# Layer 1's experts in two halves of the node tiles, with routing and last stage set between them

## The chip, the cores and the metric

The kernel runs on one core of a Trainium2 chip. The metric is the device time of one execution in microseconds. A kernel of this size has one instruction stream for each engine (TensorE, called PE; VectorE, DVE; ScalarE, ACT; GpSimd, POOL; and SyncE, SP, which issues most DMAs). Each engine works through its own stream in order and waits on semaphores for the others.

## The reference

A two-layer graph network over 6250 nodes of 256 features and 100,000 edges. Each layer adds a graph convolution and a linear attention, and then a mixture of experts. Only the last of these, layer 1's experts, has changed much:

```python
# x: (6250, 256) after layer 1's graph attention and mixer
xn = _layernorm(x)
gate_logits = xn @ gate_w + gate_b                 # 16 experts
topk_vals, topk_idx = lax.top_k(gate_logits, 2)
topk_w = softmax(topk_vals)
h = relu(einsum('bsh,ehf->bsef', xn, w1) + b1)     # 256 -> 512
expert_out = einsum('bsef,efh->bseh', h, w2) + b2  # 512 -> 256
moe = sum(topk_w * expert_out[chosen two])
y = xn + moe
x = x + (y - mean(y)) / sqrt(var(y) + EPS) * gamma + beta
```

The kernel computes only the two chosen experts of each node, in float32.

## The kernel before

Nodes lie in 49 tiles of 128 (the last has 106). Layer 1's experts are the function `expert_pairs`, in three stages one after the other.

*Routing* (`dispatch`, with `finals`, `logits` and `put`) goes over 13 groups of 2, 3 and then 4 node tiles. `finals` loads the running sum `xl` and the transposed rows `xm`, multiplies `xm` by the mixer's `kvm` (tile `mix`, L1908), divides the attention sums `acc` by their denominators (L1914), adds everything and stores the new x to `xs2_d` in DRAM. `logits` normalizes it into `xn` (one copy for each of the two choices), transposes it on PE (L131, evicted by ACT at L133) and multiplies by the router (tile `lp`, L387). `put` searches the two largest logits (`top`, `ti`, L400 and L401), counts with a scan and two products (tile `pp`, L436 and L437) which row of its expert's area each node gets (`d_pi`, L443), and scatters the rows with POOL's indirect DMA into `xs_d` (`f_xs` in the profile, L448): two scatters for each node tile. `logits` of one group is written down ahead of `put` of the group before it; the order of the engines' instructions in this stage is a scheduler's. `xn` has three buffers. During the stage SP also loads the second weights `w2` of all 16 experts (8.4 MB). At its end `dispatch` makes a table: for every expert tile of 128 rows its expert and its first row. It then writes 128 zero rows behind each expert's rows (L498): eight addresses are read into registers at once on SP, eight on ACT.

*Experts* (`stages`, `some`) go over these tiles, in an order written out by hand (`tc.manual_schedule()`). For tile i, `load` fetches the expert's first weights `w1` (512 KB, five buffers) and the rows `xt` five tiles ahead; `turn` transposes the rows two tiles ahead; `first_product` makes the 512 hidden values `hT` (16 matmul records at L1983, evicted half by ACT, L1988, half by DVE, L1991) one tile ahead; `second_product` makes `y` (8 records, L1999), DVE adds b2 and the input (L2002, L2004), and POOL scatters the result into `ys_d` (`f_ys`, L332), to the row of its node and choice. `b2` lies in `acc`, over the columns of the first 16 node tiles. Between the tiles a small generator reads `xs2_d`, adds beta and writes it back. The first 104 tiles always run; three conditional blocks of 3 follow, each run only if there are so many tiles.

*Last stage* (L2030 to L2043): in seven groups of 7 node tiles, both results and x + beta are loaded, added, normalized on DVE, scaled by gamma and written out.

Layer 0's experts use the same `dispatch` with one choice and groups of 2, 5 and 7 tiles.

Of the kernel before, what the change touches and what calls it, by code (L numbers as in the profile page):

```python
# [52 lines left out]
def gps_kernel(ctx, tc, x, src, dst, edge_weight, g0_W, g0_b, m0_WqT, m0_WkvT, m0_WpT, m0_bp,  # L53
# [276 lines left out]
    def give_back(name, ys_d, xt, y):  # L330

        st = nc.gpsimd.indirect_dma_start(  # L332
            out=ys_d, in_=y, in_offset=None,
            out_offset=bass.IndirectOffsetOnAxis(ap=xt.bitcast(I32)[:, C:C + 1], axis=0),
            bounds_check=ys_d.shape[0] - 1, oob_is_err=False)
        tc.declare_no_dep(st.ins, group=name + "y", reason="every result has a row of its own")
        tc.add_to_no_dep_group(name + "y", st.ins)

    def results(t, ys_d, k, t0, n):

        whole = n if t0 + n < NT else n - 1
        if whole < n:
            nc.vector.memset(t[:, whole, :], 0.0)
        r0 = (k * NT + t0) * P
        if whole:
            nc.sync.dma_start(t[:, :whole, :], ys_d[r0:r0 + whole * P, :].rearrange(
                "(t p) c -> p t c", p=P))
        if whole < n:
            nc.sync.dma_start(t[:LAST, whole, :], ys_d[r0 + whole * P:r0 + whole * P + LAST, :])

    def dispatch(name, fb, fw, pps, ne, nk, sizes, rw, rb, ns, xs_d, finals):
# [21 lines left out]
        def logits(t0, n):  # L373
            x_ = finals(t0, n)
            xn = [fw.tile([P, bt, rw_], F32, name=f"xn{k}", bufs=3) for k in range(nk)]
            layernorm(fw, x_, xn[0][:, :, :C], n)
            for k in range(nk):
                if k:
                    nc.scalar.copy(xn[k][:, :n, :C], xn[0][:, :n, :C])
                nc.vector.tensor_copy(xn[k].bitcast(I32)[:, :n, C], ids[:, k, t0:t0 + n])  # L380
                if nk == 2:
                    nc.vector.memset(xn[k][:, :, C + 2], 1.0 - k)
# [5 lines left out]
            lg = fw.tile([P, bt, ne], F32, name="lg")  # L388
# [4 lines left out]
        def put(t0, n, xn, lg, turn):  # L393
            ti = fw.tile([P, bt, 8], U32, name="ti")
# [59 lines left out]
        held = logits(*groups[0])  # L454
        for j, g in enumerate(groups):
            ahead = logits(*groups[j + 1]) if j + 1 < len(groups) else None
            put(*g, *held, j % 2)
            held = ahead
# [598 lines left out]
    xs2_d = tc.dram_tile([P, NT, C], F32, name="xs2_d")  # L1057
# [797 lines left out]
    def expert_pairs(ne, nk, hid, w1_d, b1_d, w2_d, b2_d, rw_d, rb_d, ns, xs_d, ys_d):  # L1855
        lead, step = 104, 3
        nf = hid // P
        wn = 2 * hid
        with ExitStack() as ctx1:
            fp = ctx1.enter_context(tc.tile_pool(name="f1", bufs=1))  # L1860
            oi = [fp.tile([1, ns], I32, name=f"own{n}") for n in (1, wn, nf, C)]
            adr = fp.tile([1, ns], I32, name="adr")
# [4 lines left out]
                                             ap=[[0, P], [1, C]]))  # L1867
            with tc.tile_pool(name="f1w", bufs=1) as wp_:
# [10 lines left out]
                with tc.tile_pool(name="f1a", bufs=2) as fw, tc.tile_pool(name="f1b", bufs=1) as fb, \  # L1879
                        tc.tile_pool(name="f1p", bufs=2, space=PSUM) as pps:  # L1880
                    rw = fb.tile([P, 2, ne], F32, name="rw")
                    nc.scalar.dma_start(rw, rw_d.rearrange("(c p) o -> p c o", p=P))
                    rb = fb.tile([P, ne], F32, name="rb")
                    nc.scalar.dma_start(rb, bass.AP(tensor=rb_d.tensor, offset=rb_d.offset,
                                                    ap=[[0, P], [1, ne]]))
                    b1 = fb.tile([ne, hid], F32, name="b1")
# [5 lines left out]
                    accv = acc.rearrange("p (t c) -> p t c", c=CR)  # L1892
                    rd = fb.tile([P, NT, 4], F32, name="rd")
                    nc.vector.tensor_scalar(rd, accv[:, :NT, C:], 1e-16, None, op0=OP.add)
                    nc.vector.reciprocal(rd, rd)

                    def finals(t0, n):
                        xl = fw.tile([P, 4, C], F32, name="xl", bufs=3)
                        nc.sync.dma_start(xl[:, :n, :], xs1_d[:, t0:t0 + n, :])
                        for t in range(t0, t0 + n, 2):  # L1900
                            m = min(2, t0 + n - t)
                            xm = fw.tile([P, 2, 2, P], F32, name="xm", bufs=4)
                            for i in range(m):
                                nc.sync.dma_start(xm[:, i], xnT_d[t + i])
                            mix = pps.tile([P, 2, C], F32, name="mix")
                            for i in range(m):
                                for h in range(2):
                                    nc.tensor.matmul(mix[:, i, h * P:(h + 1) * P], xm[:, i, h, :],  # L1908
                                                     kvm[:, h, :], start=True, stop=True)
                            i = t - t0  # L1910
                            nc.vector.tensor_add(xl[:, i:i + m, :], xl[:, i:i + m, :], mix[:, :m, :])
                        for t in range(t0, t0 + n):
                            av = accv[:, t, :C].rearrange("p (k d) -> p k d", k=4)
                            nc.vector.tensor_tensor(  # L1914
                                av, av, rd[:, t, :, None].to_broadcast([P, 4, 64]), op=OP.mult)
                        nc.vector.tensor_add(xl[:, :n, :], xl[:, :n, :], accv[:, t0:t0 + n, :C])
                        nc.sync.dma_start(xs2_d[:, t0:t0 + n, :], xl[:, :n, :])
                        if t0 >= 8:
                            for _ in range(2):
                                next(w2s, None)  # L1920
                        return xl[:, :n, :]

                    own, first, nt = dispatch("f1", fb, fw, pps, ne, nk, (2, 3) + (4,) * 11, rw, rb, ns, xs_d,
                                              finals)
                    for _ in w2s:
                        pass
                    for o, n in zip(oi, (1, wn, nf, C)):
                        nc.vector.tensor_scalar(o, own, float(n), None, op0=OP.mult)
                    nc.vector.tensor_copy(adr, first)
                    nc.vector.tensor_copy(used, nt)  # L1930
                with tc.tile_pool(name="f1x", bufs=1) as fb, tc.tile_pool(name="f1v", bufs=2) as fv, \
                        tc.tile_pool(name="f1q", bufs=2, space=PSUM) as pps:
                    b2 = acc[:, :ne * C]
                    nc.scalar.dma_start(b2, bass.AP(tensor=b2_d.tensor, offset=b2_d.offset,
                                                    ap=[[0, P], [1, ne * C]]))
                    bet = spread(fb, f1_beta, "bet")

                    def with_beta(t0):
                        xb = fb.tile([P, CH, C], F32, name="xb")
                        nc.sync.dma_start(xb, xs2_d[:, t0:t0 + CH, :])  # L1940
                        yield
                        nc.vector.tensor_tensor(xb, xb, bet[:, None, :].to_broadcast([P, CH, C]),
                                                op=OP.add)
                        yield
                        nc.sync.dma_start(xs2_d[:, t0:t0 + CH, :], xb)
                        yield

                    betas = (None for t0 in range(0, NT, CH) for _ in with_beta(t0))
# [140 lines left out]
```

## Time and profile before

| | |
|---|---|
| median of 7 runs | 3434.54 us (3425.16 to 3440.21) |
| the profiled execution | 3435.69 us, of it the span 3433.8 us |
| PE busy in the span | 2235.0 us (65%), 10357 instructions |
| DVE busy | 2217.7 us (65%), 6283 |
| POOL busy | 1938.0 us (56%), 1895 |
| ACT busy | 658.6 us (19%), 1775 |
| mean granted PE clock | 0.811 |
| HBM | 431.21 MB read, 116.99 MB written |

Times in the profile are counted from the first instruction. A line such as "L448 POOL" is line 448 of the kernel before. The profile gives, for groups of instructions, their busy time, the mean of one, and the idle time of their engine just before them with the instruction that ended it; in such rows "out<-in" names the tiles written and read. The "chain" is followed back from the last instruction through whatever released each step. PE's clock is granted by the chip between 0.50 and 1.00 of full speed and is given as a mean over a stretch. A float32 matmul shows as two records, a transpose as one. The DMA share is the mean busy share of the core's 16 DMA engines.

### The profile page before, as it was taken

The page shows a single profiled execution, that of the slowest core. Times are in us where ns is not written, and L with a number is a line of the kernel's source. Part 1 is how long each engine was busy: PE and PEld are TensorE (multiplying, and loading weights), DVE is VectorE, ACT ScalarE, POOL GpSimd, SP SyncE. Part 2 cuts the span into 40 slices and gives each one's busy share as a digit, 9 for nine tenths or more (in the row PEclk, how much of TensorE's full clock was granted, in tenths as well). Part 3 has the DMA queues.
Part 4 walks back from the last instruction along what each step waited for, and adds up shares of the span by engine and source line. Part 5 has one row for each costly group of instructions (what it writes and reads, how often), then busy time and mean ns, then how long its engine had stood idle before and what let it go on. Part 6 is the DMA issues. An engine that isn't in the chain of part 4 may idle for free. (4 is left out here: it accounts for less than half of the span.)

```text
span 3433.8 us, 40629 instructions
## 1 busy us (share of the span) xinstructions
PE 2235.0 (65%) x10357; PEld 1708.9 (50%) x10357; DVE 2217.7 (65%) x6283; ACT 658.6 (19%) x1775; POOL 1938.0 (56%) x1895
## 2 busy tenths in 40 slices
PE   4677789985555364767455556555555564999970
PEld 3444567764434253656233334333333453899970
DVE  6365666666666673665478888788888764344448
ACT  2212112210000011422011111111111132344420
POOL 0477777777777433710677777777777055222220
PEclk9989999997677655988788888888877665999995
DMA  6734434433333325466655555555554384777757
GB/s 199 210 115 122 117 117 126 128 114 99 95 96 95 99 60 134 153 212 181 189 165 160 161 160 167 165 167 159 169 164 122 103 285 144 241 254 251 249 183 246
DMA packets 323374, 547.51 MB, mean 159 GB/s; under 512 B 83881, under 2 KB 208274, under 8 KB 322995
## 3 DMA queue, kind: packets, MB, share of 16 engines
q1 hardware_dynamic: 224556, 285.05, 26.1%
q0 software_dynamic: 91104, 245.32, 24.7%
q10 hardware_dynamic: 7464, 14.32, 1.4%
q8 instruction: 94, 1.54, 0.2%
q14 instruction: 156, 1.28, 0.1%
HBM read 431.21 MB, written 116.99 MB: 160 GB/s over the span
## 5 line engine op out<-in xcount | busy, mean ns | idle before, releaser
L300 POOL DMA_INDIRECT h<-h_d,idx x782 | 785.7, 1005 | 404.7 <-issue 229.8
L300 POOL DMA_INDIRECT xg<-xw_d,idx x782 | 803.4, 1027 | 364.5 <-issue 222.7
L1547 PE MATMUL ps<-h,S 128*128 128x260 f32 x1564 | 416.4, 429 | 426.6 <-DVE S L1541 426.6
L852 PE MATMUL ps<-xg,S 128*128 128x256 f32 x1564 | 489.6, 458 | 268.5 <-DMA xg<-xw_d,idx 197.5
L1547 PEld LDWEIGHTS ps<-h,S 128*128 128x128 f32 x1564 | 329.7, 215 | 520.8 <-DVE S L1541 463.4
L852 PEld LDWEIGHTS ps<-xg,S 128*128 128x128 f32 x1564 | 334.0, 228 | 393.0 <-issue 184.2
L332 POOL DMA_INDIRECT f_ys<-y,xt x175 | 184.8, 1056 | 361.6 <-DVE y L2004 273.4
L860 DVE SCALAR_TENSOR_TENSOR acc<-ps,in,acc 128x256 f32 x392 | 188.3, 480 | 281.8 <-PE ps L852 280.6
L448 POOL DMA_INDIRECT f_xs<-xn,d_pi x147 | 152.4, 1037 | 194.0 <-DVE d_pi L443 80.5
L1536 DVE TENSOR_TENSOR h<-h,exi 128x2048 f32<-128x2048 f32 x98 | 223.0, 2276 | 57.1 <-ACT exi L1495 57.1
L850 DVE TENSOR_SCALAR S<-iota,lo,wt 128x128 f32<-128x128 f32 x782 | 240.4, 356 | 0.1
L1991 DVE TENSOR_SCALAR h<-hT,b1T 128x128 f32<-128x128 f32 x214 | 75.1, 351 | 218.1 <-ACT h L1988 217.7
L1983 PE MATMUL hT<-xTt,w 128*128 128x128 f32 x1712 | 209.9, 276 | 0.3 <-ACT xTt L133 0.3
L1999 PE MATMUL y<-w,h 128*128 x856 | 202.1, 379 | 0.0
L1983 PEld LDWEIGHTS hT<-xTt,w 128*128 128x128 f32 x1712 | 201.0, 193 | 0.6 <-ACT xTt L133 0.5
L1404 PE MATMUL p<-ST,hw 128*32 128x512 f32 x392 | 177.4, 606 | 34.7 <-DVE ST L1399 16.9
L1999 PEld LDWEIGHTS y<-w,h 128*128 128x128 f32 x856 | 154.6, 190 | 16.7
L1495 ACT ACT_TABLE_LOAD x24 | 30.8, 1283 | 466.2 <-DVE z L1492 465.9
L1541 DVE TENSOR_TENSOR S<-exi,lo 128x1024 f32<-128x1024 f32 x98 | 118.8, 1212 | 1.0 <-ACT h L1538 1.0
L1404 PEld LDWEIGHTS p<-ST,hw 128*32 128x32 f32 x392 | 41.6, 112 | 156.0 <-issue 116.1
L131 PE MATMUL tr<-ident,xt 128*128 128x128 f32 x350 | 70.1, 284 | 71.4 <-DMA xt<-f_xs 71.4
L1988 ACT ACTIVATE h<-hT,b1T 128x128 f32<-128x128 f32 x214 | 78.7, 368 | 152.5 <-PE hT L1983 103.9
(347 smaller groups left out, 3862.7 us busy)
## 6 DMA issues: line engine op xcount, KB each, us to landing
w<-in_L_ffn_w SPq DMA_DIRECT2D x123, 512.0 KB
ST<-lob_d SPq DMA_DIRECT2D x97, 512.0 KB
xt<-f_xs SPq DMA_DIRECT2D x107, 129.5 KB
xnT<-xT SPq DMA_DIRECT2D x98, 128.0 KB
xT<-xnT SPq DMA_DIRECT2D x98, 128.0 KB
xg<-xw_d,idx POOLq DMA_INDIRECT x782
h<-h_d,idx POOLq DMA_INDIRECT x782
xt<-f_xs SPq DMA_DIRECT2D x68, 128.5 KB
```

Of the source, the lines that this page charges most:

```text
L300: return nc.gpsimd.indirect_dma_start(out=o, out_offset=None, in_=tab, in_offset=bass.IndirectOffsetOnAxis(ap=idx, axis=0))
L332: st = nc.gpsimd.indirect_dma_start(out=ys_d, in_=y, in_offset=None, out_offset=bass.IndirectOffsetOnAxis(ap=xt.bitcast(I32)[:, C:C + 1], ...
L448: st = nc.gpsimd.indirect_dma_start(out=xs_d, in_=xn[k][:r, i, :], in_offset=None, out_offset=bass.IndirectOffsetOnAxis(ap=pi[:r, t, k:k + ...
L850: nc.vector.tensor_scalar(S[:, i, :], iota, lo0[:, t:t + 1], wt0[:, t:t + 1], op0=OP.is_equal, op1=OP.mult)
L852: users.append([nc.tensor.matmul(ps, S[:, i, :], xg[:, i, :], start=i == 0, stop=i == n - 1) for i in range(n)])
L860: nc.vector.scalar_tensor_tensor(a, ps, m[:, b:b + 1], a, op0=OP.mult, op1=OP.add)
L1404: nc.tensor.matmul(p4[:, :w], hw[:, i, :], ST[:, j * P:j * P + w], start=i == 0, stop=i == nj - 1)
L1536: nc.vector.tensor_tensor(v, v, ex[:, u:u + m, :, None].to_broadcast([P, m, 4, 64]), op=OP.mult)
L1541: nc.vector.tensor_tensor(S[:, :m, :], iop[:, None, :].to_broadcast([P, m, P]), lo1[:, t0 + u:t0 + u + m, None].to_broadcast([P, m, P]), o ...
L1547: users[t0 + u][i] = nc.tensor.matmul(ps, S[:, i, :], h8[:, i, :], start=i == m - 1, stop=i == 0)
L1983: nc.tensor.matmul(hT[:, f, :], w1[:, c, f * P:(f + 1) * P], xT[:, c, :], start=c == 0, stop=c == 1)
L1999: nc.tensor.matmul(yp, h[:, f, :], w2e[:, f * C:(f + 1) * C], start=f == 0, stop=f == nf - 1)
```

## The change

The nodes are parted after 25 node tiles (`HT`, the first seven groups). Routing becomes a class `Routing` whose methods are generators: each `yield` ends a *step*. The parts run in this order:

1. The first 25 node tiles are routed, under the scheduler, with the logits of two groups ahead and four `xn` buffers. A table is made of the first `LA` = 42 expert tiles, from *full* tiles only, whose rows are all written.
2. These 42 tiles run, by hand. Their row loads don't wait for the scatters of the second half. Between a tile's products an object `Beside` takes steps of the second half's routing, 1.9 for each call, two calls a tile, from the second tile on. At its end come the table of the second run (up to 78 tiles) and the zero rows, whose 16 addresses are now read one at a time, all on SP.
3. `LB` = 65 tiles run, by hand. From tile `due_a` = 24 on, when all tiles with rows of the first half are through, steps of the first half's last stage are taken between the products (1.2 a call), and beta is added to the second half's x (0.3 a call), which stays in `acc` and no longer goes through DRAM. Two conditional blocks, of 4 and the rest, follow.
4. The last stage for the other 24 node tiles, in marks of 4, with ACT rather than DVE normalizing.

`xt` has seven buffers instead of eight. In layer 0's `dispatch`, too, the logits of two groups are held ahead, and the ids are written into `xn` in `put` rather than in `logits`. The diff, cut to its core:

```diff
@@ dispatch (both layers before, layer 0 alone after) @@
-            xn = [fw.tile([P, bt, rw_], F32, name=f"xn{k}", bufs=3) for k in range(nk)]
+            xn = [fw.tile([P, bt, rw_], F32, name=f"xn{k}", bufs=2 + nk) for k in range(nk)]
...
-        held = logits(*groups[0])
+        held = [logits(*g) for g in groups[:2]]
         for j, g in enumerate(groups):
-            ahead = logits(*groups[j + 1]) if j + 1 < len(groups) else None
-            put(*g, *held, j % 2)
-            held = ahead
+            put(*g, *held.pop(0), j % 2)
+            if j + 2 < len(groups):
+                held.append(logits(*groups[j + 2]))
@@ expert_pairs @@
-        lead, step = 104, 3
+        bt, HT, LA = 4, 25, 42
+        LB, step = 65, 4
+        FA = HT * P * nk // P
+        nb = ns - (FA - ne + 1)
+        due_a = FA - LA + ne
...
+        class Beside:
+            def step(self):
+                self.due += self.rate
+                while self.due >= 1.0 and self.gen is not None:
+                    self.due -= 1.0
+                    try:
+                        next(self.gen)
...
+                def logits(self, g):
+                    x_ = yield from self.sums(g)
...
+                    for k in range(1, nk):
+                        nc.scalar.copy(xn[k][:, :n, :C], xn[0][:, :n, :C])
+                    self.loads(g + 1 + self.deep)
+                    lp = self.psum("lp", [P, bt, ne])
+                    last = None
+                    for i in range(n + 1):
+                        xT = transposed(fw, self.pps, xn[0][:, i, :C], "xT") if i < n else None
+                        if last is not None:
+                            for c in range(2):
+                                nc.tensor.matmul(lp[:, i - 1, :], last[:, c, :], rw[:, c, :],
+                                                 start=c == 0, stop=c == 1)
+                        last = xT
+                        yield
+                    lg = fw.tile([P, bt, ne], F32, name="lg", bufs=2 + self.deep)
+                    nc.vector.tensor_tensor(lg[:, :n, :], lp[:, :n, :],
+                                            rb[:, None, :].to_broadcast([P, n, ne]), op=OP.add)
+                    return xn, lg
...
+                def put(self, g, xn, lg):
+                    for k in range(nk):
+                        nc.vector.tensor_copy(xn[k].bitcast(I32)[:, :n, C], ids[:, k, t0:t0 + n])
...
+                    for i in range(n):
+                        nc.vector.max(top[:r, i, :], lg[:r, i, :])
+                        nc.vector.max_index(ti[:r, i, :], top[:r, i, :], lg[:r, i, :])
+                    yield
...
+                    nc.vector.tensor_tensor_scan(flat(s), flat(mask), flat(c), 0.0,
+                                                 op0=OP.mult, op1=OP.add)
+                    pp = self.psum("pp", [P, ne, bt])
+                    nc.tensor.matmul(pp, before, c[:, :, 1:], start=True, stop=False)
+                    nc.tensor.matmul(pp, ones, s[:, :, :bt], start=False, stop=True)
+                    yield
...
+                    held = [drain(route.logits(g)) for g in range(2)]
+                    for g in range(ga):
+                        drain(route.put(g, *held.pop(0)))
+                        if g + 2 < ga:
+                            held.append(drain(route.logits(g + 2)))
+                            for _ in range(3):
+                                next(w2s, None)
...
+                    def some(tiles, tab, beside=None, start=0, free=False):
+                        steps = stages(tiles, tab, free)
                         for i in range(tiles[0] - 5, tiles[-1] + 1):
                             for ahead, do in steps:
                                 if tiles[0] <= i + ahead <= tiles[-1]:
                                     do(i + ahead)
+                                if beside is not None and ahead in (1, 0) and i >= start:
+                                    beside.step()
...
+                            for e in range(ne):
+                                for r in group_values(tail, e, SP, ne * CAP - P, 1):
+                                    st = nc.sync.dma_start(xs_d[ds(r, P), :], zero[:, :rw_])
...
+                    def ends(first, count, fw, at_once):
+                        loads(0)
+                        yield
+                        for j, (t0, n) in enumerate(marks):
+                            loads(j + 1)
...
+                            for i in range(n):
+                                nc.scalar.activation(xc[:, i, :], xc[:, i, :], AF.Identity,
+                                                     bias=rs[:, 1, i:i + 1], scale=rs[:, 0, i:i + 1])
...
+                    with tc.manual_schedule(engines={PE, ACT, DVE, SP}):
+                        half = Beside(second_half(), 1.9)
+                        some(range(LA), tabs[0], half, 1, True)
+                        half.rest()
+                        rest = Beside(first_ends(), 1.2)
+                        betas = Beside(with_beta(), 0.3)
...
+                        some(range(LB), tabs[1], Both(), due_a)
+                        rest.rest()
+                        betas.rest()
...
+                    with tc.If(have[0] > LB):
+                        some(range(LB, LB + step), tabs[1])
+                        with tc.If(have[0] > LB + step):
+                            some(range(LB + step, nb), tabs[1])
+            with tc.tile_pool(name="f1f", bufs=3) as fw:
+                drain(ends(HT, NT - HT, fw, 1))
```

One group of four node tiles takes 23 steps of routing: two for `mix`, three for the sums, five for the normalization, five for transposes and router products, one for the logits' sum, one for the search, one for the count with `pp`, one for the rows `d_pi`, and four of scatters.

## The prediction

> **What bounds the kernel now.** I read four views in this order: busy time by stage, the chain of waits, POOL's timeline, and the groups by line. Only the last 720 us of the span are touched, so I start with the stage table (length, then busy us of PE, PEld, DVE, ACT and POOL with instruction counts, granted PE clock, DMA share, GB/s).
>
> ```profile
> 2714.00:2927.00 213.00, 108.53 (x562) 99.77 (x563) 123.16 (x644) 66.50 (x114) 99.37 (x98) 0.58 0.68 221
> 2927.00:3316.00 389.00, 389.00 (x2702) 362.57 (x2701) 178.97 (x421) 157.17 (x415) 111.13 (x103) 1.00 0.73 243
> 3316.00:3334.00 18.00, 11.82 (x80) 10.53 (x78) 5.75 (x14) 3.93 (x11) 4.80 (x5) 0.95 0.06 22
> 3334.00:3434.00 100.00, 0.00 (x0) 0.00 (x0) 79.08 (x177) 3.38 (x8) 0.00 (x0) 0.50 0.73 256
> ```
>
> Routing (213 us) fills no engine; the experts (389 us) are PE alone, without a gap, at clock 1.00; the last stage (100 us) is DVE alone. So the two outer stages could lie beside the middle one, if PE has room, and it has none: whatever PE work or PE wait routing brings along lengthens the middle. The chain of waits gives the joints (start, length, what):
>
> ```profile
> 2910.25 6.94 DMA f_xs<-xn,d_pi
> 2921.54 5.02 DMA xt<-f_xs
> ...
> 3288.93 1.79 PE hT L1983 x16
> 3292.66 1.79 PE hT L1983 x16
> ...
> 3324.60 9.53 DMA f_ys<-y,xt
> 3334.94 6.96 DMA yg<-f_ys
> 3342.31 2.04 DVE xc L2036
> ```
>
> One expert tile takes 3292.66 - 3288.93 = 3.73 us. From the last scatter's start (2910.25) to the first expert product (2927.3) are 17.0 us; from PE's end (3328) to the last stage's first addition (3342.3) 14. In routing, POOL's timeline shows the pace (in brackets the idle time before):
>
> ```profile
> 2808.11 0.97 POOL L448 DMA_INDIRECT f_xs<-xn,d_pi  x1 [5.42 <-DVE d_pi L443]
> 2824.64 0.97 POOL L448 DMA_INDIRECT f_xs<-xn,d_pi  x1 [6.53 <-DVE d_pi L443]
> 2833.67 0.97 POOL L448 DMA_INDIRECT f_xs<-xn,d_pi  x1 [0.30 <-issue]
> ```
>
> A group's eight scatters are 1.28 us apart, then POOL waits 4 to 6.5 us for the next group's rows (d_pi). The scatter at 2833.67 is the last of the seventh group: 25 of 49 tiles.
>
> **The change part by part.**
>
> *Tile count.* Before ran 104 tiles and one block of 3, so there are 105 to 107. Counted with the reference on its inputs: 106 tiles, and the first 25 node tiles hold exactly 42 full ones. So after runs 42 and 65 (64 real): again 107, both conditional blocks skipped.
>
> *Layer 0's routing* gets its products two groups ahead. In the built program DVE's order differs only in the first and last group. Nothing, then. Bounds: the 31.9 us that DVE waits there for lp, as a gain; 32.4 us as a loss, what DVE waits in layer 1 for an xn buffer. It is nearest to neither: 0.
>
> *First half's routing before the experts.* At the old pace its last scatter starts at 2833.7. Two groups ahead and a fourth xn buffer attack the 32.4 us in 8 waits of DVE for f_xs. Bounds: no gain, or six gaps of 5.5 us gone (33 us). But the DMA share in 2714 to 2822 is already 0.84, and all 16 w2 loads fall there again, so I take 8: 2826. The table of 42 tiles, some 25 DVE operations of 0.14 to 0.27 us, lies beside the last eight scatters (10.2 us); without that cover it costs 6. With 17.0 us the experts start at 2843 rather than 2927: 84 us off.
>
> *First 42 expert tiles with the second half's routing.* The tiles: 42 x 3.73 = 157. Routing's PE work for 24 tiles at clock 1.00: four mix records as hT's (1.79 / 16 = 0.112), two transposes of 0.192 (40.6 us over 212), four router records bound by their weight load as hT's (201.0 / 1712 = 0.117), 1.3 us a tile, 31; and pp, 24 records of 0.12: 34 in all. The other bound is the durations that these lines had in routing (mix 0.237, lp 0.196, tr 0.262, pp 0.28): 61. I take 34, as the stage is near full load.
>
> Then PE's waits. Engines run in order, and a call of the interleaver, two for each tile, makes about two steps, so PE meets operands that DVE has only begun. Worst is pp: ahead of it DVE adds lg (0.22) and y (0.42 + 0.48), writes ids (0.44), searches four tiles and counts:
>
> ```profile
> L401 DVE FIND_INDEX8 ti<-top,lg 128x8 uint32<-128x16 f32 (+1 forms) x49 | 7.7, 169 | 0.0
> L400 DVE MAX8 top<-lg 128x8 f32<-128x16 f32 (+1 forms) x49 | 6.0, 162 | 0.0
> L434 DVE TENSOR_TENSOR_SCAN d_cum<-d_mask,d_cnt 128x80 f32<-128x80 f32 x13 | 4.1, 315 | 0.0
> L401 DVE MATCH_VALUE_LOAD ti<-top,lg 128x8 f32 (+1 forms) x49 | 3.7, 76 | 0.0
> ```
>
> 4 x (0.169 + 0.162 + 0.076) = 1.63, and 1.4 for kf, df, oh, two d_cnt and the scan: 4.6 us. In the built order four of six groups have only y's product ahead of pp, and PE stands some 4.5 us; the others 3.5 and 1.9: 23. Router transposes behind ACT's copy of xn (1.05) and of xT (0.37): four groups x 1.3, and 3 in small ones: 8. The second table: 4. Sum 35. ACT has 101 us (66.5 / 49 a routed tile, 1.62 an expert tile), DVE 128 (123.2 / 49 and 1.61), POOL 115 (48 scatters and 42 returns of 1.28): all below PE's time. 157 + 34 + 35 = 226.
>
> *The clock.* Whether waits of 4.5 us cost clock too is seen in layer 0's experts, with work between them as well:
>
> ```profile
> 1380.00:1400.00 20.00, 15.27 (x92) 12.38 (x91) 12.35 (x33) 8.38 (x23) 12.64 (x12) 0.92 0.60 189
> 1400.00:1420.00 20.00, 19.70 (x143) 17.59 (x143) 10.88 (x35) 12.30 (x35) 14.75 (x15) 0.99 0.58 180
> 1420.00:1440.00 20.00, 9.87 (x52) 7.76 (x51) 13.74 (x12) 4.96 (x14) 15.82 (x6) 0.78 0.27 88
> ```
>
> PE busy 76% has 0.92, 98% has 0.99. With PE busy in 191 of 226 us (85%) I read about 0.95 to 0.97; 5 us more: 231. Bounds: 191 without waits, 290 in the second rival.
>
> The Trainium skill speaks against the change here: its page "TensorE: Matmul & The Clock Gate" (section "Why this matters for your kernels") advises no PE gap over about 3 us between bursts, since one idle window brings the half clock back. If each of five pp waits were followed by 3.4 us of half clock, the page's window, that would add 8 us where I add 5; the rows above show the mean clock and not the single gap.
>
> *The joint.* The second table's d_tail product stands ahead of two first products, three second ones and a transpose, 10 us of PE. Then SP reads 16 registers one by one, each followed by its zero write; before, eight came from one read. A read and its issue take 1.3 us (at the start of the experts 0.81 from a read to its issue, and 0.34, with gaps): 21 us. Behind them in SP's queue stand the second run's w1 and xt: 2.5 us for reads and issues, 5.0 for xt to land, 1 to the first product. 1 + 21 + 8.5 - 10 = 20 us that PE stands; bounds 14 (0.9 each, as the old writes) and 28. Two more for the clock's return (first product 2.94 us, then 1.79): 22.
>
> *65 tiles with the first half's last stage.* 65 x 3.73 = 243. From tile 24 on DVE has 1.61 us a tile for the experts (172.4 us over 107), 7.4 x 2.4 / 11 = 1.61 for the ends (7.4 for a mark of four: eight wide operations of 0.60, by 2.02 for 1792 columns against their 512, four statistics of 0.40, 1.0 of small ones; 11 steps, 2.4 a tile), and 0.36 for beta: 3.58 of 3.73. The DMA rises from 210 GB/s (243 less 33 for the old beta pass) by 0.87 x 524 KB / 3.73 us = 123 to 333, where 0.84 of the engines moved 281. Both nearly full for 31 tiles. Bounds 0 and 24 (a tenth on each); I take 8: 251. SP waits at every mark for xc's output to land before the next loads, with w1 and xt queued behind; five tiles (18.7 us) are loaded ahead, which hides some 5 us; with that cover gone it costs PE that much a mark.
>
> *Last stage of 24 tiles.* 12 us from PE's end to the first addition (14, with loads of 512 for 896 KB); six marks of 6.2 us (no beta), and 1 each for ACT's round trip, as normalizing moves there: 43; 8 from the last addition to the end (3425.7 to 3433.8, as before). 63 rather than 106.
>
> **Sum.** 2843 + 231 + 22 + 251 + 63 = 3410 against the span of 3433.8, 24 us less. The profiled run took 3435.7 and the median is 3434.5: **3411**.
>
> **Rivals.**
> 1. *PE's waits vanish in the interleaving.* If DVE runs far enough ahead of PE that most operands lie ready, the first stage is 200, the joint 14 + 2, the second run 247: 3410 - 31 - 6 - 4 = **3369**. For it: DVE's 128 us of 200 leave it a third of slack. Against it: pp's chain is serial in its step. 22%.
> 2. *The clock falls in the first 42 tiles.* At 0.76, as where layer 0's experts were half busy, 191 us of PE work become 251, with waits 286: 3410 + 55 = **3465**, slower. For it: 0.58 in routing. Against it: 0.92 at 76% busy. It decides once the stage takes over 255 us, 6.1 a tile. 17%.
> 3. *DVE and DMA bound the second run.* 31 tiles at 10% more on each is 24 rather than 8: **3426**, no change. 10%.
>
> **How the numbers follow.** My forecast, 51%, covers 3390 to 3426 by the bounds of joint and first half. Range 3355 to 3455: below it lies part of the first rival, above it much of the second. What differs by under 0.2% (7 us) can't be told from no change. Faster: 51 + 22 = 73%; same 10; slower 17.
>
> **What would show it.** First product at about 2843; 42 tiles in about 231 us at clock 0.95, with PE waits of 3 to 5 us on d_cnt; 20 us without PE between two runs, SP busy with 16 reads; slots of 3.7 to 4.1 us while first results are written; 63 us after PE's end. I am wrong if the first stage takes under 210 or over 255, or the joint is under 10.

## The result and the profile after

The changed kernel takes 3453.53 us (median of 19 runs, 3447.81 to 3464.33), the kernel before beside it 3435.28 (46 runs). The ratio is 1.0056, with a 95% interval from 1.0046 to 1.0065: slower by about 18 us, where 24 less were forecast. The profiled execution is one of the longer ones, with a span of 3460.4 us. On three of the five chips used below (the first four experiments, the eighth to the tenth, and the last two) every kernel took 3760 to 4070 us, the one before included; there, stretches between named events are compared, kernel against kernel, and not whole runs.

The busy time by stretch of the changed kernel (start and end, length, busy us of PE, PEld, DVE, ACT and POOL with instruction counts, granted PE clock, DMA share, GB/s). The rows are the first half's routing, the first 42 tiles up to the first zero write, the joint, the 65 tiles, and the last stage:

```profile
2714.00:2829.20 115.20, 59.97 (x301) 55.30 (x302) 66.92 (x358) 34.27 (x60) 50.40 (x50) 0.56 0.74 251
2829.20:3103.20 274.00, 217.09 (x1329) 196.57 (x1329) 132.54 (x504) 91.88 (x216) 87.75 (x87) 0.86 0.50 160
3103.20:3127.40 24.20, 11.63 (x57) 10.04 (x57) 4.13 (x10) 2.25 (x6) 2.95 (x3) 0.71 0.58 187
3127.40:3386.80 259.40, 249.16 (x1680) 229.67 (x1680) 148.67 (x384) 110.10 (x291) 66.43 (x63) 0.97 0.72 237
3386.80:3460.40 73.60, 1.84 (x9) 1.28 (x7) 37.44 (x105) 14.23 (x30) 1.96 (x2) 0.53 0.57 185
```

Routing stood alone for 213 us before; now its first half does for 115. But the second row should be PE alone, as the experts were before (389 of 389 us, clock 1.00). PE is idle in it for 274.0 - 217.1 = 56.9 us, and its clock is 0.86. No other engine is full there: DVE works 132.5 of 274 us. The last row has no full engine at all: DVE 37.4 of 73.6.

What ended PE's waits in the second row (engine and line, what it waited for; us in all, times, longest):

```profile
PE gm L2066 <- DVE d_cnt L2061: 19.8, 6, 3.5
PE tr L131 <- DVE xn L2001: 18.1, 6, 4.4
PE gm L2016 <- ACT xT L133: 10.2, 7, 2.9
PE gm L1964 <- DMA xm<-xnT: 3.2, 1, 3.2
```

Each of the first three comes about once a group, of six groups. One group in PE's order of time (start, duration; in brackets the idle time before the instruction, and what ended it):

```profile
2974.75 1.95 PE L2255 MATMUL hT<-xTt,w 128*128 128x128 f32 x16
2978.68 0.73 PE L131 MATMUL tr<-ident,xn 128*128 128x128 f32 x4 [1.98 <-DVE xn L2001]
2981.43 1.04 PE L2016 MATMUL gm<-rw,xT 128*128 128x16 f32 x4 [2.01 <-ACT xT L133]
2982.30 3.76 PE L2271 MATMUL y<-w,h 128*128 x8
...
2988.63 3.25 PE L2255 MATMUL hT<-xTt,w 128*128 128x128 f32 x16
...
2997.53 0.44 PE L2066 MATMUL gm<-d_cnt,before 128*128 128x64 f32 x2 [3.48 <-DVE d_cnt L2061]
...
2998.57 3.39 PE L2255 MATMUL hT<-xTt,w 128*128 128x128 f32 x16
3001.80 1.89 PE L2271 MATMUL y<-w,h 128*128 x8
```

A `y` takes 1.89 us and an `hT` 1.95 in this view when nothing is wrong. Behind two waits of 2 us a `y` takes 3.76 and the next `hT` 3.25; behind the wait for the count an `hT` takes 3.39. The granted clock in the first of these (2982.30 to 2986.00) is 0.50. Two more places of the same row:

```profile
2837.39 1.95 PE L2255 MATMUL hT<-xTt,w 128*128 128x128 f32 x16
2842.59 1.16 PE L1964 MATMUL gm<-kvm,xm 128*128 128x128 f32 x8 [3.25 <-DMA xm<-xnT]
2843.59 1.89 PE L2271 MATMUL y<-w,h 128*128 x8
...
3075.16 1.95 PE L2255 MATMUL hT<-xTt,w 128*128 128x128 f32 x16
3079.78 0.43 PE L2066 MATMUL gm<-d_cnt,before 128*128 128x64 f32 x2 [2.66 <-DVE d_cnt L2061]
3080.14 0.69 PE L2067 MATMUL gm<-d_cum,ones 128*128 128x64 f32 x2
3080.62 3.38 PE L2271 MATMUL y<-w,h 128*128 x8
```

A single wait of 2.66 us is followed by slow products too, and the wait of 3.25 us for `xm` is not: it is the one exception in this row among the waits of over 2.5 us and the pairs of some 2 us. The others are followed by some microseconds at about half the clock. Two theories lead into the experiments. *Clock*: this loss is real, some 30 us besides the waits. *DVE sets the pace*: PE is only as fast as DVE hands over operands, and its low clock goes along with that.

### The profile page after: what moved, and what is told of

The parts are those of the page before. It is cut to its first block, busy times and chain, and to the rows that moved or that the text cites. A ratio compares the mean times of both kernels' runs of the same rounds, so it can differ in the third digit from the quotient of the medians.

```text
span 3460.4 us, 40722 instructions
## 1 busy us (share of the span) xinstructions
PE 2280.9 (66%) x10385; PEld 1739.7 (50%) x10385; DVE 2222.4 (64%) x6393; ACT 679.6 (20%) x1830; POOL 1929.0 (56%) x1895
## 5 line engine op out<-in xcount | busy, mean ns | idle before, releaser
L856 PE MATMUL ps<-xg,S 128*128 128x256 f32 x1564 | 498.8, 465 | 256.6 <-DMA xg<-xw_d,idx 184.2
L2255 PE MATMUL hT<-xTt,w 128*128 128x128 f32 x1712 | 227.8, 291 | 2.7 <-ACT xTt L133 2.7
L2255 PEld LDWEIGHTS hT<-xTt,w 128*128 128x128 f32 x1712 | 218.4, 207 | 3.7 <-ACT xTt L133 3.5
L2271 PE MATMUL y<-w,h 128*128 x856 | 219.2, 403 | 1.2 <-DVE h L2263 1.2
L2271 PEld LDWEIGHTS y<-w,h 128*128 128x128 f32 x856 | 165.8, 204 | 22.2 <-DVE h L2263 1.7
L2085 POOL DMA_INDIRECT f_xs<-xn,d_pi x98 | 99.1, 1011 | 114.1 <-DVE d_pi L2079 55.9
```

The source lines that it names most:

```text
L856: users.append([nc.tensor.matmul(ps, S[:, i, :], xg[:, i, :], start=i == 0, stop=i == n - 1) for i in range(n)])
L2085: st = nc.gpsimd.indirect_dma_start(out=xs_d, in_=xn[k][:r, i, :], in_offset=None, out_offset=bass.IndirectOffsetOnAxis(ap=pi[:r, t, k:k + ...
L2255: nc.tensor.matmul(hT[:, f, :], w1[:, c, f * P:(f + 1) * P], xT[:, c, :], start=c == 0, stop=c == 1)
L2271: nc.tensor.matmul(yp, h[:, f, :], w2e[:, f * C:(f + 1) * C], start=f == 0, stop=f == nf - 1)
```

## The experiments

**Filling the waits.** In the second half's routing alone, products that nobody reads are written into unused columns of the routing's own PSUM tile: 13 ahead of the first router transpose, 7 ahead of the first router product, 15 ahead of the count's product, in each group.

```diff
+                            def fill(n):
+                                for _ in range(n):
+                                    nc.tensor.matmul(raw[0][:, 256:384], ident, before,
+                                                     start=True, stop=True)
...
+                    self.fill(15)
                     nc.tensor.matmul(pp, before, c[:, :, 1:], start=True, stop=False)
```

> After's kernel with 35 extra products of 128x128 for each of the six routing groups beside the first 42 tiles, put on PE just ahead of the three instructions that wait (13 ahead of the first router transpose, 7 ahead of the first router product, 15 ahead of the count product), into unused columns; by the first products' own 1.79 us for eight such products that is 0.224 each, 7.8 us a group, 47 in all, about what PE stood there (48). Theory 'clock': the waits of 2 to 3.5 us bring the half clock, and that is some 35 us of the stage's 284; filled, tiles go back to 1.8 us a product and the stage falls to about 247, the run to about 3417. Rival 'waits alone' (the stage is paced by DVE's chain, the low clock only goes along with it): stage 284 or more, run 3454 or more.

The run took 3964.9 us beside 3905.14 before, on a chip where every kernel took longer. The stretch from first product to first zero write was 301.5 us there; the third experiment, which leaves this stretch as it is, took 316.3 on the same chip.

> The kernel of the first experiment again (35 extra products for each routing group ahead of the three instructions that wait), on another chip, as all runs beside the first were some 14% longer than usual, the kernel before among them. Theory 'clock': stage of the first 42 tiles about 247 us instead of 284, run about 3417, ratio to before 0.995. Rival 'waits alone': 284 or more, ratio 1.005 or more.

Here the kernel before took 3447.48 us and this one 3446.97: ratio 1.0006 (0.9988 to 1.0024). Its row from first product to first zero write:

```profile
2832.20:3084.40 252.20, 236.49 (x1750) 221.44 (x1749) 132.72 (x504) 91.85 (x216) 88.10 (x87) 0.97 0.54 173
```

The stretch falls from 274.0 to 252.2 us although PE has 421 records more. One of these takes 0.117 us (3.51 us for 30 of them ahead of a count), so they are 49 us; without them PE is busy for 236.5 - 49.2 = 187.3, not 217.1. So the half clock had cost about 29.8 us, and the clock is back at 0.97. The idle time falls from 56.9 to 15.7. Net: 49.2 - 29.8 - 41.2 = -21.8. DVE does not set the pace: it did the same work in 22 us less. The two runs on one chip, 301.5 against 316.3, point the same way. The run's gain is 0.5% where the theory asked for 1%: it had put the slow clock at 35 us and all 48 us of the three waits as filled, by 47 us of products, where 29.8, 41.2 and 49.2 were measured.

**The same work behind the waits.** As above, with each block of extra products put after the instruction that waits. The block behind the first router transpose thus stands ahead of the first router product.

```diff
                     nc.tensor.matmul(pp, ones, s[:, :, :bt], start=False, stop=True)
+                    self.fill(15)
```

> The same 35 extra products for each group, but put right behind the three waiting instructions instead of ahead of them, so that the waits stay. Theory 'clock': 47 us at full clock and up to twice that right behind a wait, so the stage goes from 284 to 330 or 345, the run to about 3505. Rival 'paced by DVE': PE work added behind a wait shortens the next wait by as much, the stage stays under 300 and the run under 3470.

> The second experiment again (35 extra products for each routing group right behind the three waiting instructions, so that the waits stay), on a chip where the kernel before takes its usual time. In the fifth experiment an extra product took 0.117 us for each of its two records, so the extra work is 49 us at full clock, and put into the waits it shortened the stretch from the first expert product to the first zero write from 274 to 252. Theory 'clock': behind the waits the same work runs partly at half clock and hides nothing: 274 + 49 to 274 + 75, that is 323 to 349, the run about 3510. Rival 'paced by DVE': what is added behind one wait is taken off the next, the stretch stays under 290.

> The extra products behind the waits once more, where the kernel before takes its usual time. On the two other chips they lengthened the stretch from first product to first zero write from 316 to 352, by 36 of their 49 us, the same both times. Theory 'clock and waits': 274 + 36 to 274 + 49, that is 310 to 323; ahead of the waits the same work gave 252. Rival 'paced by DVE': under 290.

All three fell on chips where everything took longer: ratios 1.026 (1.0091 to 1.0429), 1.0267 (1.018 to 1.0354) and 1.0253 (1.0139 to 1.0366). The stretch took 351.9, 351.9 and 348.9 us; the unchanged stretch took 316.3 (the third experiment), 315.9 (the ninth) and 323.0 (the fourteenth), each on the same chip as one of them. So the same work that saves time in the waits costs 26 to 36 us behind them, less than the 49 of the clock theory, more than the 16 of its rival. On the first experiment's chip all three can be seen side by side: 316.3 unchanged, 301.5 with the products in the waits, 351.9 with them behind. The eighth experiment's PE in order of time:

```profile
3326.26 1.97 PE L2275 MATMUL y<-w,h 128*128 x8
3331.71 0.69 PE L2069 MATMUL gm<-d_cnt,before 128*128 128x64 f32 x2 [3.48 <-DVE d_cnt L2064]
3332.20 0.63 PE L2070 MATMUL gm<-d_cum,ones 128*128 128x64 f32 x2
3332.62 5.93 PE L2305 MATMUL gm<-before,ident 128*128 128x128 f32 x30
3338.39 0.38 PE L131 MATMUL tr<-ident,xt 128*128 128x128 f32 x2
3338.61 1.95 PE L2259 MATMUL hT<-xTt,w 128*128 128x128 f32 x16
```

The wait is still 3.48 us. The extra products pay for the slow clock behind it (5.93 us for 30 records rather than 3.51), and the `hT` that follows, 3.39 above, is back at 1.95. Why the whole cost is under 49 is seen beside the ninth experiment, on the same chip. PE is busy 40.8 us more (276.4 against 235.6), so the loss by the slow clock is some 8 us smaller. And it is idle 4.8 us less, as the block ahead of the first router product fills the wait for `xT` (0.2 us, against 9.4).

**Fewer steps to a call.** The same routing in 12 steps a group, one for each call, so that PE meets what DVE and ACT made a call earlier.

```diff
-                        half = Beside(second_half(), 1.9)
+                        half = Beside(second_half(), 1.0)
```

> After's kernel with the same routing work beside the first 42 tiles in 12 steps a group, one in each call of the interleaver, instead of 23 steps, 1.9 in each call: whatever PE reads was made by DVE or ACT one call (1.8 us of expert products) earlier. Theory 'clock and waits': hardly a wait over 1 us is left, the clock stays at about 0.97, 157 of tiles and 34 of routing and some 14 of rest make the stage about 205, and the run about 3375. Rival 'paced by DVE, POOL or DMA': the stage stays over 250 and the run over 3420.

The run took 3921.17 us, ratio 1.0167 (1.0063 to 1.0271), on the third experiment's chip. The stretch took 281.9 us rather than that run's 316.3: a gain of 34, far from the 80 hoped for. ACT in order of time, there:

```profile
3403.47 0.30 ACT L2143 ACTIVATE ln_sd<-ln_mv,eps 128x4 f32<-128x4 f32 x1 [3.58 <-DVE ln_mv L2142]
3403.67 0.35 ACT L133 COPY xTt<-tr 128x256 f32<-128x256 f32 x1
3403.92 0.51 ACT L2325 ACTIVATE xf<-xt 128x256 f32<-128x256 f32 x1
3407.66 0.37 ACT L2339 ACTIVATE h<-hT,b1T 128x128 f32<-128x128 f32 x1 [3.23 <-remote]
```

The normalization's root waits 3.58 us for DVE, and the expert tile's copy `xTt` stands behind it in ACT's queue. On PE the waits for the count fall to 9.5 us in 6, but those of the router transposes for DVE's `xn` grow to 44.7 us in 6, more than half of the 65.6 us that PE is idle. The second wait above, by a releaser that the profile does not name, seems to belong to the chip: such waits add up to 30.4 us in 6 in the fourteenth experiment's stretch, and the changed kernel's profile has none.

**The steps piped.** One group's sums and statistics beside the products, search and count of the group before, again 12 calls a group, with no call meant to hold over 1.5 us of DVE work. The calls also begin two expert tiles sooner (the start -1 instead of 1).

```diff
+                            for g in range(ga, len(groups)):
+                                ahead = route.early(g + 1, x_) if g + 1 < len(groups) else iter(())
+                                for _ in route.later(g, x_.pop(g)):
+                                    next(ahead, None)
+                                    yield
...
-                        half = Beside(second_half(), 1.9)
-                        some(range(LA), tabs[0], half, 1, True)
+                        half = Beside(second_half(), 1.0)
+                        some(range(LA), tabs[0], half, -1, True)
```

> The same routing work beside the first 42 tiles in 12 steps a group, one in each call, as in the fourth experiment, but a group's sums and statistics now stand beside the group before's products, search and count, so that no call has more than 1.5 us of DVE work (there, four calls in a row had 1.6 to 2.1, and ACT's root stood ahead of the expert tile's copy). Theory 'clock and waits': 157 of tiles, 34 of routing and some 14 of rest make the stage about 205, the run about 3375, ratio 0.983. Rival 'paced by DVE, POOL or DMA': stage over 250, ratio over 0.996.

3415.62 us beside 3447.48, ratio 0.9903 (0.9873 to 0.9933). PE between two counts (some records left out):

```profile
2921.75 0.43 PE L2074 MATMUL gm<-d_cnt,before 128*128 128x64 f32 x2 [0.92 <-DVE d_cnt L2067]
...
2935.60 0.44 PE L131 MATMUL tr<-ident,xt 128*128 128x128 f32 x2 [0.30 <-ACT xT L133]
...
2950.84 0.43 PE L2074 MATMUL gm<-d_cnt,before 128*128 128x64 f32 x2 [0.92 <-DVE d_cnt L2067]
```

A group with its six expert tiles takes 29.1 us where the changed kernel took 42.0 (2955.52 to 2997.53, counts again): 22.4 for the tiles, 5.5 of routing, 1.2 of waits, at clock 1.00 (the changed kernel's 42.0 had 0.84). This pace is that of one group and does not come from the sooner start. The stretch is 222.0 us, not 205, as the second table and the zero writes follow after the last group, and beside few tiles (PE busy 11.2 us of 20, clock 0.70). The rival is out: DVE, POOL and DMA carry this pace.

**Loads twice.** The diff shows `loads(j + 1)` at each mark of the last stage; behind it stands, for the last 24 tiles alone, `loads(j + 2)`. Nothing keeps a mark from being asked for twice.

```diff
-                            if j >= len(marks):
+                            if j >= len(marks) or j in come:
                                 return
+                            come.add(j)
```

> After's kernel, but in the last stage each mark of four tiles is loaded once: after's loop asks for mark j+1 and j+2 at every mark, so the last four of six marks are loaded twice (ten loads of yg and ten of xc for six marks, 4.2 MB more than the 6.3 MB wanted). Theory 'double loads': DVE's waits for yg (18.3 us in 4) fall by about half, the last stage goes from 72 to about 63, the run to 3444. Rival 'order of SP' (the loads stand behind the writes of out, and would be late in any case): 72 as before, 3453.

3936.97 us, ratio 1.0179 (1.007 to 1.0288), on a chip where everything took longer. The stretch from the last first product to the end is 61.1 us (3783.6 to 3844.7), against 75.5 in the changed kernel and 75.4, 73.6 and 74.5 in the three other runs on this chip. The changed kernel's tile `yg` in its last stage (duration least, median and most; first and last start), and what DVE waited for:

```profile
L348 SPq DMA_DIRECT2D yg<-f_ys x10: 359/507/1702, 3396.3 to 3437.1; - x10
...
L351 SPq DMA_DIRECT2D yg<-f_ys x2: 244/560/875, 3430.3 to 3439.6; - x2
...
  DMA yg<-f_ys: 18.3, 4
```

and in the seventh experiment, which loads once:

```profile
L348 SPq DMA_DIRECT2D yg<-f_ys x6: 360/440/1317, 3346.5 to 3361.7; - x6
...
L351 SPq DMA_DIRECT2D yg<-f_ys x1: 340/340/340, 3366.7 to 3366.7; - x1
...
  DMA yg<-f_ys: 10.4, 1
```

Six marks need six whole loads, not ten. With the double ones gone, one wait for `yg` is left, that for the first load.

**Piped, loaded once, zero writes on two queues.** SP and ACT take eight of the sixteen each; the rest as in the two experiments above.

```diff
-                                for r in group_values(tail, e, SP, ne * CAP - P, 1):
-                                    st = nc.sync.dma_start(xs_d[ds(r, P), :], zero[:, :rw_])
+                                eng, q = ((SP, nc.sync), (ACT, nc.scalar))[e % 2]
+                                for r in group_values(tail, e, eng, ne * CAP - P, 1):
+                                    st = q.dma_start(xs_d[ds(r, P), :], zero[:, :rw_])
```

> The sixth experiment's kernel, and with it each mark of the last stage loaded once, and the sixteen zero writes at the joint put on two queues, eight by SP and eight by ACT. If the three add up: 13 us less in the last stage (the difference of the first three experiments' last stages to that of the third's), 7 less at the joint (half of 14.7), so 20 under the sixth experiment, about 3355, ratio 0.977. Rival: the last stage and the joint are set by transfers behind them, and the run is as the sixth experiment's within 5 us.

> The seventh experiment's kernel again (routing in 12 steps a group, marks loaded once, zero writes on two queues), beside the twelfth on one chip. Where the kernel before takes its usual 3435 to 3450 us: ratio 0.986 as there, a first run of 42 tiles of 220 us from first product to first zero write, and 58 us behind the last product. Rival 'the seventh was a lucky chip': ratio over 0.995.

3398.49 us beside 3447.48, ratio 0.9859 (0.9832 to 0.9887), and on another chip 3382.95 beside 3430.98, 0.9862 (0.9845 to 0.9879). The gains add up nearly: 17.1 us under the sixth experiment of 20 forecast. Of these, 14.2 lie in the last stage (58.1 us against 72.3). The zero writes take 7.9 and 8.4 us, side by side, instead of 13.8, but PE still waits 18.0 us for `xt` at the joint, where the sixth experiment waits 20.4: what is saved in writing is mostly not saved in landing.

**The table ahead of the last tiles.** The first group's sums and statistics are made before the first expert tile, so that everything ends some calls sooner.

```diff
-                            for j, _ in enumerate(route.early(ga, x_)):
-                                if j % 2:
-                                    yield
+                            drain(route.early(ga, x_))
+                            yield
...
                         half = Beside(second_half(), 1.0)
+                        next(half.gen)
```

> The seventh experiment's kernel with the first of the six groups' sums and statistics done ahead of the first expert tile, in the time in which PE waits for its first rows (23 us there), so that the routing needs 6 calls less and the second table and the sixteen zero writes end some 3 tiles before the 42nd instead of behind it. If the joint is set by table and zero writes, PE's 15 us wait for xt at the joint goes and the stretch of the table's own waits (8 us) lies further ahead: about 12 us under the seventh experiment, 3386, ratio 0.982. Rival: the first expert tile comes later by as much (DVE has 6 us of the early work ahead of its first addition): ratio as the seventh's, 0.986.

3809.73 us, ratio 0.9967 (0.9915 to 1.002), on a chip where everything took longer, without a seventh beside it: no gain or loss can be read from it. But SP stood some 9 us (3184.1 to 3192.7) ahead of the second group's loads, with the first tile's weights queued behind them. With these moved behind the first tiles' loads:

> The tenth experiment's kernel with the loads of the second of the six groups issued behind the first expert tiles' loads (there SP stood 10 us with them, until the first group's sums had freed their buffer, with the first weights and rows queued behind). If the joint is set by the table and the zero writes, these now end some 3 tiles ahead of the 42nd, PE's 15 to 18 us wait for xt at the joint goes, and the run is about 12 us under the eleventh's. Rival: the early sums hold up the first expert tiles by as much, and both runs are equal within 4 us.

3367.77 us beside 3430.98, ratio 0.9822 (0.9805 to 0.9839), 15.2 us under the eleventh. PE's waits at its joint:

```profile
PE hT L2347 <- ACT xTt L133: 6.3, 1, 6.3
PE tr L131 <- DMA xt<-f_xs: 1.6, 2, 1.1
```

The wait for `xt` is 1.6 us where the eleventh experiment has 17.4. The 6.3 are new: ACT's eight zero writes stand ahead of an expert tile's copy. This is the fastest of the kernels tried, faster than the kernel before and the changed one.

**The first half's last stage behind the 65 tiles.**

```diff
                         class Both:
                             def step(self):
-                                rest.step()
                                 betas.step()
```

> After's kernel, but the first half's last stage (25 node tiles) stands behind the second run of 65 expert tiles instead of beside it; only the beta additions stay beside it. Theory 'beside it costs PE some 15 us': the 65 tiles take 245 us instead of 260 (65 x 3.73 = 243), and the stage behind them gets the 25 tiles, 7 marks of about 7.5 us, 50 us more: run about 3490. Rival 'the 65 tiles are late for other reasons (loads, the clock after the joint)': 260 as before, run about 3505.

> After's kernel with the first half's last stage behind the 65 tiles, once more. On the other chip the stretch from the first zero write to the last first product fell from 281 to 264. Theory 'the last stage beside the tiles takes 18 us from PE': 264 here as well, the stage behind 111 us instead of 75, the run about 18 us over after's, ratio 1.011. Rival: a stretch of 275 or more, as that chip's was disturbed.

Ratios 1.0195 (1.0108 to 1.0283) and 1.0176 (1.008 to 1.0273) to the kernel before; the changed kernel itself did not run on these two chips. The fourteenth experiment's rows for joint with 65 tiles, and for the last stage:

```profile
3589.50:3854.20 264.70, 252.10 (x1735) 234.52 (x1735) 113.52 (x278) 99.73 (x264) 65.64 (x66) 0.97 0.70 212
3854.20:3962.20 108.00, 1.78 (x9) 1.22 (x7) 78.99 (x220) 30.12 (x63) 2.16 (x2) 0.53 0.67 218
```

The changed kernel has 24.2 + 259.4 = 283.6 and 73.6. The last stage beside the tiles takes 19 us from them, and saves 34 behind them. That the first sum depends little on the chip is seen in the third experiment (282.4) and the eighth (283.9).

## Why the prediction was wrong

The direction was wrong, and nearly all of it in one step. The time lies inside the range of 3355 to 3455 by its width alone. Luck hid part of the miss: the 42 tiles, the 65 tiles and the last stage took 53, 8 and 11 us more than forecast, but the first half and the joint 14 and 8 us less. By the steps of the sum:

- *First half's routing*: 2843 forecast, 2829.2 measured. The last scatter starts at 2818.53 rather than 2826, and from there to the first product are 10.7 us rather than 17. The step came 14 us sooner: the routing's first `mix` starts 5 us earlier (2716.6 against 2721.9), more of the scatters' gaps went than I took, and why the rest after the last scatter is shorter was not looked into.
- *The 42 tiles and the joint*: 231 + 22 = 253 forecast, 274.0 + 24.2 = 298.2 measured; counted to the end of their products (3113.5), the 42 tiles took 284 us rather than 231. **This is the step that failed.** The work was nearly right (191 forecast; 187.3 lies ahead of the first zero write, 10.4 at clock 0.80 behind it). The waits ahead of that write were 56.9 us, not 35. The count's own term was close (19.8 against 23). But the 8 us that I had put for transposes and products of the router were all behind ACT's copies. The products' wait for `xT` was 10.2, and the transposes waited 18.1 us more for DVE's normalization (`xn`), a wait that I had put at nothing. And the clock cost about 29.8 us where I had put 5. For this I had read rows of 20 us of layer 0's experts (76% busy at 0.92) and carried over their mean; even of the 0.95 to 0.97 so read, 5 us is only what 0.97 makes of 191, and 0.95 makes 10. PE was 79% busy here too (217.1 of 274), at 0.86. So the idle share alone does not give the clock; in order of time, the slow products lie behind the waits. My bound from 191 to 290 us held the outcome. My second rival, 3465 with a fall of the clock, was the case that came about, but its 286 us for the stage are close by two misses: it had 35 us of waits and 60 by the clock. (The row that it names has 0.78, not 0.76.)
- *The joint* alone was about 14 us when counted from the end of the 42 tiles' products (3113.5) to the first `hT` of the second run, where I forecast 22: a read and its zero write take 0.92 us (14.69 for sixteen), not 1.3.
- *65 tiles*: 251 forecast, 259.4 measured. The term of 8 us for DVE and DMA beside PE was 18 to 19 by the ninth and fourteenth experiments, inside its bounds of 0 and 24.
- *Last stage*: 63 forecast from PE's end, 71.7 measured from there (73.6 in the row above, which starts 1.9 us sooner). I had sized the loads without seeing in the code that four of six marks are asked for twice; that is some 14 us. Loaded once, the stage takes 58 to 60 us (58.1 in the seventh experiment, 59.5 in the eleventh).
- *Layer 0's routing* at nothing: no effect is seen. Layer 1's first `mix` starts at 2716.6 us rather than 2721.9, but the fifth, sixth, seventh, eleventh and twelfth experiments, with the same code up to there, have it anywhere from 2710 to 2737.

The Trainium skill's advice against PE gaps of over about 3 us (page "TensorE: Matmul & The Clock Gate", section "Why this matters for your kernels") pointed the right way. I had weighed it at 8 us. The trace is harsher than this limit: a single gap of 2.66 us, and two of 1.98 and 2.01 us with 0.7 us of work between them, are followed by slow products as well. In one place it is milder, where the gap of 3.25 us is not.

The first rival, that waits vanish when DVE runs far enough ahead, is what the piped routing made true: it gave a group at 29.1 us and clock 1.00, and the twelfth experiment, with the other repairs, a ratio of 0.9822 (this rival's 3369 would be 0.981). The idea of the change held; its 23 steps at 1.9 a call did not.

## What to carry to other kernels

Work set between the instructions of an engine that is full must be cut so that each operand is made a whole call before that engine meets it, and the other engines' queues must not hold the main work's copies behind the added work's waits. Price each wait on PE twice, once for itself and once for the slow clock that followed nearly every longer one here; products put into the wait show the second price directly. When a stage in which no engine is full gets longer, count its loads before looking for contention.

## What the hardware showed that was not expected

- The clock's return is quick, and not always in the same place: behind one wait of 3.48 us an `hT` takes 3.39 us and the `y` after it 1.89, behind another (before 2955.52) an `hT` 2.86 and its `y` 2.69.
- Products that nobody reads, in the waits, kept the clock at 0.97 and made the stretch 21.8 us shorter, with 49 us more work on PE.
- On some chips the same stretch took 316 to 323 us instead of 274, with waits on ACT whose releaser the profile cannot name (30.4 us in 6 in the fourteenth experiment); what causes them was not found.
